# A 17-tap convolution by 48-point transforms of 32-node blocks, in batches of 16 graphs, in a two-layer graph network

## The chip, the cores and the metric

The kernel runs on one core of a Trainium2 chip, in one launch, all in f32. The time is that of the launch on the device in microseconds (us); the median of several runs is compared. PE is TensorE (matmuls), DVE is VectorE, ACT is ScalarE, POOL is GpSimd, and SP is the engine whose queue issues nearly all DMAs here.

## The reference

There are 64 graphs of 256 nodes with 256 features. Layer 0, with batch norms folded to a scale and a shift per channel:

```python
xc = transpose(x)                                   # channels x nodes
h = relu(bn1(conv1d(xc, conv1_w, taps=1)))
h = bn2(conv1d(h, conv2_w, taps=17, pad=8))         # along the nodes
x_conv = transpose(relu(h + xc))
s = x @ w_se.T + b_se                               # 3 numbers a node
A = exp(-(|s_n|^2 + |s_m|^2 - 2 s_n.s_m)) * adj
x_nmp = A @ relu(x @ w_msg.T + b_msg)
x_in = concat(x_conv, x_nmp)                        # 512 features
r, z, n = GRU gates of (x_in @ w_ih.T, x @ w_hh.T)  # sigmoid, sigmoid, tanh
x = layernorm(x + (1 - z) * n + z * x)
```

Layer 1 is `h = layernorm(x)`, `x + relu((adj @ h) @ W_rel + h @ W_root + b)`, and a last layernorm.

## The kernel before

**Pairs.** Graphs are worked on two at a time, 32 pairs. `pair(p)` loads the transposed x of both graphs (xT, line 1055) and the adjacency (adjm, 1058), makes messages (ps_msg, 1073) and distances (ps_dist, 1107), takes the exponential, multiplies it by the mask on VectorE (1114), and makes the neighbour sum nmp (1121). The conv result xc gets x added on VectorE (1127) and its relu on ScalarE (1128). Lines 1139 to 1142 form sums and differences of quarters of xT, nmp and xc on VectorE: the gate products (1155, by far the most of PE's work) are 2 x 2 block products done with 7 instead of 8 multiplications, except in the three pairs of `PLAIN`. Then follow the gates (1222 to 1231), transposes back (ps_wT, 1252), the norm's few small GpSimd operations (1265 to 1274), the projection (ps_hy, 1285), the aggregate (ps_agg, 1299) and the last norm (1310 to 1329). In the pairs of the last batch (`late`) the norms' sums come from VectorE's `bn_stats`; in others, from ScalarE with an accumulated output.

**The convolution** is done in batches of `BG` = 8 graphs. `conv1(b)` transposes x, stores it for later (xt), multiplies by conv1's matrix (828) and applies batch norm and relu (832). For batches after the first, the result goes to DRAM (hd) and comes back as XF (842). Each graph is cut into blocks of M = 16 nodes, and for each the T = 32 points of a cyclic transform over the block and its neighbouring nodes are taken: `fold` (767) makes the sums U and the differences V of halves, `split` (589 to 608) turns V and U down to points, each a pair re, im of [128 channels x 256] per channel half. At each of 15 complex points the conv is a product of 256 x 256 matrices, by three real products (lines 703 and 720 to 722): with the sum of re and im, with re, with im. Two real points need one each. That makes `NM` = 3 x 15 + 2 = 47 matrices. `merge` (619 to 643) and the last steps (878 to 886) go back up; ACT applies the second batch norm and writes the result to XC in SBUF (892).

The 47 matrices come from the 17 taps once, in `filters()`: a GpSimd copy lays 7 output channels together (ws, 538), PE turns them (544), multiplies by a constant matrix of cosines and sines (561, `NM * OB` = 329 columns), and ACT copies the result to W2 in SBUF (564). `store_w2` writes them to DRAM (w2m). Batch 0 multiplies straight from W2; later batches load three matrices a time (768 KB, line 696) into one of two places in `cs`.

**Order.** The program is first recorded as operations, each with a key (a wished time): `FIRST_GATES + p * PERIOD` for the gates of pair p, and a span of time over which the conv of the next batch is spread. `scheduled` plays a list schedule with estimated durations, giving each engine the ready operation with the lowest key, and the engines' queues are written in the order that comes out. It counts a DMA as 1.6 us plus its bytes by 205 KB/us, one after another. On the chip each engine runs its queue strictly in that order, SP too. PSUM has 8 banks, of which conv products may hold 3.

Of the kernel before, what the change touches and what calls it, by code (L numbers as in the profile page):

```python
# [18 lines left out]
P = 128  # L19
# [11 lines left out]
M, T = 16, 32  # L31
BG = 8
# [12 lines left out]
V0, U, S, S2, SLOTS = 0, 16, 32, 40, 48  # L45
HP_LEN = M * C * BG * (M + 1)

LEAVES = [(V0 + k, V0 + 8 + k, a) for k, a in enumerate(leaf_angles(PI / 2, 8))]
LEAVES += [(U + 8 + k, U + 12 + k, a) for k, a in enumerate(leaf_angles(PI / 2, 4))]
LEAVES += [(U + 4 + k, U + 6 + k, a) for k, a in enumerate(leaf_angles(PI / 2, 2))]  # L50
LEAVES += [(U + 2, U + 3, PI / 2)]
NM = 3 * len(LEAVES) + 2
SR, LR = 32, 100
OB = 7
HQ = 2 * M * C * (M + 1)
XC_SLOTS = BG + 2
FIRST_GATES, PERIOD, GATE_TIME = 143.0, 60.5, 18.0
AHEAD_FROM, AHEAD_TO, W_DEEP = -20.0, 10.0, 2
CONV1_FROM, CONV1_TO, CONV_FROM, CONV_OUT, CONV_TO = -10.0, 120.0, -6.0, -70.0, -30.0
PAIR_LEAD, FILTER_LEAD, LOAD_AHEAD = 20.0, 15.0, 12.0  # L60
# [3 lines left out]
def tap_matrix():  # L64

    k = np.arange(TAPS)
    cols = []
    for _, _, a in LEAVES:
        c, d = np.cos(k * a) / (T / 2), -np.sin(k * a) / (T / 2)
        cols += [c, d - c, c + d]  # L70
    cols += [np.ones(TAPS) / T, (-1.0) ** k / T]
    return np.stack(cols, 1).astype(np.float32)
# [177 lines left out]
DRAM_UNIT = P * D  # L250


def dram_cells(ap):

    name = ap.tensor.name
    if not name.startswith(("w2m", "xt", "hd")):
        return []
    dims = list(ap.ap)
    top = ap.offset + sum(s * (n - 1) for s, n in dims)
    return [(name, u) for u in range(ap.offset // DRAM_UNIT, top // DRAM_UNIT + 1)]  # L260

# [45 lines left out]
def scheduled(ops):  # L307
# [38 lines left out]
    while todo:  # L346
# [34 lines left out]
        if op.moved:  # L381
            dma = max(dma, now + 1.6) + op.moved / 205e3
# [23 lines left out]
def gnn_two_layers(  # L406
# [51 lines left out]
    cs = sb("cs", [P, W_DEEP * 3 * C * D])  # L458
    xn_ahead = sb("xn", [P, HQ])
    xn_ahead.base.fine = 0  # L460
    xTc_ahead = sb("xTc", [P, C, 2 * N])
# [5 lines left out]
    XF = sb("XF", [P, S * D + HP_LEN])  # L467
    XF.base.fine = S * D
    X = XF[:, :SLOTS * D].rearrange("p (s e) -> p s e", e=D)
    HP = XF[:, S * D:].rearrange("p (q j c g k) -> p q j c g k", q=BG // 2, j=M, c=C, g=2)  # L470
    w2m = tc.dram_tile([NM, C, P, D], F32, name="w2m")
    h_dram = tc.dram_tile([B // 2, 5, P, D], F32, name="hd")
    xt_dram = tc.dram_tile([B // 2, P, C, 2 * N], F32, name="xt")
    W2 = sb("w2all", [P, C, NM, D], "first")
# [31 lines left out]
    def store_w2(c):  # L506
        for f in range(0, NM, 8):
            g = min(f + 8, NM)
            SP.dma_start(out=w2m[f:g, c].rearrange("f p o -> p f o"), in_=W2[:, c, f:g, :])

    def filters():
        pieces, groups = [], []
        for c in range(C):
            for o0, o1 in ((0, 12 * OB), (12 * OB, 24 * OB), (24 * OB, D)):
                starts = [min(o, D - OB) for o in range(o0, o1, OB)]
                for a in range(0, len(starts), 4):
                    groups.append((len(pieces), starts[a:a + 4]))
                pieces.append((c, o0, o1))
        WT, TT = {}, {}
        WS, AHEAD = {}, 4  # L520
        wts = ring("wt", [P, TAPS, D - 24 * OB], 2, "filters")
        wss = ring("ws", [P, 4, TAPS, OB], AHEAD, "filters")
        tTs = ring("tT", [TAPS * OB, 4, P], 2, "filters")
# [29 lines left out]
        for i, (piece, starts) in enumerate(groups):  # L553
# [3 lines left out]
            if i + 1 < len(groups):  # L557
                TT[i + 1] = turned(i + 1)
            for a, o in enumerate(starts):
# [4 lines left out]
                A.copy(W2[:, c, :, o + skip:o + OB], pv[:, :, skip:])  # L564
# [47 lines left out]
    def merge(re, im, size, phi, scales, tmp, joint):  # L612
# [10 lines left out]
        else:  # L623
            joint = joint and h == 2
            for v in (slice(0, 2),) if joint else (0, 1):
                for j in range(2):
                    rho = scales[1][j] / scales[0][j]
                    a2, b2 = a[:, v, j::2], b[:, v, j::2]
                    stt(tt[:, v, j::2], b2, -rho, a2)
                    yield cost(h if joint else h // 2)  # L630
                    stt(a2, b2, rho, a2)
                    yield cost(h if joint else h // 2)
# [21 lines left out]
    TREES = [(V0, V0 + 8, 8), (U + 8, U + 12, 4), (U + 4, U + 6, 2)]  # L654
# [34 lines left out]
    w2_at = cycle(range(W_DEEP))  # L689

    def load_w(b, first, n):
        if b == 0:
            return lambda m, c: W2[:, c, first + m, :]
        at = next(w2_at) * 3 * C * D
        t = cs[:, at:at + 3 * C * D].rearrange("p (m c o) -> p m c o", m=3, c=C)
        SP.dma_start(out=t[:, :n], in_=w2m[first:first + n].rearrange("f c p o -> p f c o"))
        return lambda m, c: t[:, m, c, :]

    def product(ps, slot, w, m, first=True):
        with prog.group():  # L700
            for o in range(C):
                for c in range(C):
                    PE.matmul(ps[:, o * P:(o + 1) * P], w(m, c)[:, o * P:(o + 1) * P], X[:, slot, c * P:(c + 1) * P],  # L703
                              start=first and o == 0 and c == 0, stop=(c == C - 1), skip_group_check=True)

    def products(b, first, sums):
# [4 lines left out]
        for k in range(2):  # L711
            w = load_w(b, 3 * (first + k), 3)
            at = slice(k * D, (k + 1) * D)
            product(p1[:, at], sums + k, w, 0)
            product(p2[:, at], re + k, w, 1)
            product(p3[:, at], im + k, w, 2)

        def take():
            k1 = sl(sums, 2).rearrange("p s e -> p (s e)")
# [5 lines left out]
    def products_added(first, sums):  # L725
        p1, p3 = (bank(f"ps_k{i}", "conv") for i in (1, 3))
        re, im, _ = LEAVES[first]
        w = [load_w(0, 3 * (first + k), 3) for k in range(2)]
        at = [slice(k * D, (k + 1) * D) for k in range(2)]
        k1 = sl(sums, 2).rearrange("p s e -> p (s e)")  # L730
        for k in range(2):
            product(p1[:, at[k]], sums + k, w[k], 0, k == 0)
# [715 lines left out]
```

## Time and profile before

| what | us |
|---|---|
| median of 3 runs (2084.39 to 2088.04) | 2087.75 |
| the profiled execution's own time | 2085.32 |
| its span in the trace | 2083.5 |
| first gate matmuls (ps_g) in a run of their own | 151.4 |
| last DVE step of the first batch's conv (line 886) begins | 143.1 |
| conv products: records from `cs`, from W2 | 2632, 376 |
| SP waiting at line 1055 (load of xT) for DVE line 1229 | 220.5 |

The profile is one execution. Its page has the engines' busy shares, the span in 40 slices, the chain of work that ended last, groups of instructions by line and operation, and DMA issues. Further views are the timeline of an engine, the waits, and a table of busy time by stretches. An f32 matmul stands in the trace as two records.

### The profile page before, as it was taken

How to read it: one execution, taken by the hardware profiler on the slowest of the kernel's cores; microseconds unless marked ns; L12 is line 12 of the kernel's file. 1: busy time of each engine (PE TensorE's matmuls, PEld its weight loads, DVE VectorE, ACT ScalarE, POOL GpSimd, SP SyncE). 2: the span in 40 equal slices, each digit the busy share in tenths (PEclk: the TensorE clock that was granted, in tenths of full speed). 3: DMA queues.
4: the chain of work that ended last, by engine and by line, in shares of the span. 5: the costliest groups of instructions: out<-in, count | busy, mean ns of one | idle time of the engine just before them, and what ended most of it. 6: DMA issues, size and time to landing. Idle time of an engine off the chain costs nothing.

```text
span 2083.5 us, 28847 instructions
## 1 busy us (share of the span) xinstructions
PE 2048.0 (98%) x10492; PEld 1664.2 (80%) x10492; DVE 1685.8 (81%) x3028; ACT 1018.1 (49%) x2216; POOL 317.2 (15%) x555
## 2 busy tenths in 40 slices
PE   9989999999999999999999999999999999999996
PEld 6868779778887788878888788877888779887775
DVE  7983898899868998789868998689887899875644
ACT  7443433754447544564436544464445544365432
POOL 4100210122111201111101121112011220011101
PEclk9989999999999999999999999999999999999999
DMA  7734363334423244224433245232442225211100
GB/s 211 262 98 144 124 208 112 118 102 141 161 81 120 92 160 141 94 92 141 165 107 113 72 139 170 96 112 91 159 138 83 76 74 161 75 50 53 41 21 31
DMA packets 208201, 241.19 MB, mean 116 GB/s; under 512 B 23749, under 2 KB 192700, under 8 KB 208060
## 3 DMA queue, kind: packets, MB, share of 16 engines
q1 hardware_dynamic: 207518, 238.92, 35.6%
q8 instruction: 83, 1.36, 0.3%
q14 instruction: 58, 0.48, 0.1%
q10 hardware_dynamic: 542, 0.43, 0.1%
HBM read 177.85 MB, written 61.47 MB: 115 GB/s over the span
## 4 chain that ended last, share of the span: by engine, by line
PE 94%; DVE 4%; issue 1%; ACT 0%; POOL 0%; ACTq 0%; POOLq 0%; DVEq 0%
PE ps_a L1155 21%; PE ps_k L703 16%; PE ps_d L1155 11%; PE ps_hy L1285 11%; PE ps_msg L1073 5%; PE ps_agg L1299 5%; PE ps_c L828 5%; PE ps_b L1155 5%; PE ps_g L1155 5%; PE ps_nmp L1121 4%; PE ps_w L561 2%; PE ps_wT L1252 1%; PE ps_xTc L807 1%; PE ps_dist L1107 1%; DVE RG L1230 1%
## 5 line engine op out<-in xcount | busy, mean ns | idle before, releaser
L703 PEld LDWEIGHTS ps_k<-XF,cs 128*128 128x128 f32 x2632 | 313.2, 192 | 13.0 <-issue 6.6
L703 PE MATMUL ps_k<-XF,cs 128*128 128x128 f32 x2632 | 315.4, 275 | 0.0
L1285 PE MATMUL ps_hy<-wrr,wT 128*128 128x512 f32 x512 | 226.8, 595 | 0.0
L1285 PEld LDWEIGHTS ps_hy<-wrr,wT 128*128 128x128 f32 x512 | 96.6, 191 | 107.0 <-issue 102.1
L1169 ACT ACTIVATE RG<-ps_a,bhh 128x512 f32<-128x512 f32 x116 | 79.5, 686 | 191.0 <-PE ps_a L1155 129.4
L1155 PE MATMUL ps_a<-tx,WB 128*128 128x256 f32 x522 | 156.7, 382 | 0.0
L1167 ACT COPY ZN<-ps_a 128x512 f32<-128x512 f32 x116 | 67.6, 583 | 156.5 <-PE ps_a L1155 156.2
L1287 DVE SCALAR_TENSOR_TENSOR HY<-ps_hy,q,hrow 128x512 f32<-128x512 f32 x128 | 95.8, 749 | 55.8 <-PE ps_hy L1285 41.1
L675 DVE TENSOR_TENSOR XF<-XF 128x512 f32<-128x512 f32 (+3 forms) x128 | 126.4, 1010 | 5.3 <-ACT XF L756 3.0
L1073 PE MATMUL ps_msg<-wms,xT 128*128 128x260 f32 x512 | 124.7, 384 | 0.0
L1299 PE MATMUL ps_agg<-HY,adja 128*128 128x256 f32 x512 | 119.1, 380 | 4.0 <-issue 3.5
L1121 PE MATMUL ps_nmp<-AT,msg 128*128 128x256 f32 x512 | 118.8, 380 | 3.0 <-DVE AT L1114 3.0
L1299 PEld LDWEIGHTS ps_agg<-HY,adja 128*128 128x128 f32 x512 | 96.3, 190 | 31.3 <-issue 16.1
L1073 PEld LDWEIGHTS ps_msg<-wms,xT 128*128 128x128 f32 x512 | 95.3, 190 | 19.1 <-issue 5.8
L1121 PEld LDWEIGHTS ps_nmp<-AT,msg 128*128 128x128 f32 x512 | 95.4, 190 | 18.8 <-DVE AT L1114 4.2
L828 PE MATMUL ps_c<-xTc,w 128*128 128x512 f32 x232 | 107.7, 594 | 0.5 <-ACT xTc L808 0.5
L1155 PEld LDWEIGHTS ps_a<-tx,WB 128*128 128x128 f32 x522 | 95.1, 191 | 14.0 <-issue 1.5
L1155 PE MATMUL ps_a<-tc,WB 128*128 128x256 f32 x348 | 103.8, 380 | 0.0
L1155 PE MATMUL ps_a<-xc,WB 128*128 128x256 f32 x348 | 103.6, 379 | 0.0
L1155 PE MATMUL ps_a<-tn,WB 128*128 128x256 f32 x348 | 103.5, 379 | 0.0
L1155 PE MATMUL ps_a<-nmp,WB 128*128 128x256 f32 x348 | 103.5, 379 | 0.0
L1265 POOL TENSOR_SCALAR total<-total 128x4 f32<-128x4 f32 x28 | 15.5, 552 | 544.9 <-ACT x L1261 544.9
(213 smaller groups left out, 4642.7 us busy)
## 6 DMA issues: line engine op xcount, KB each, us to landing
cs<-w2m SPq DMA_DIRECT2D x105, 768.0 KB, 4.8
adjm<-in_adjT_dram SPq DMA_DIRECT2D x64, 256.0 KB, 2.8
xT<-xt SPq DMA_DIRECT2D x32, 512.0 KB, 3.7
adja<-in_adjT_dram SPq DMA_DIRECT2D x64, 256.0 KB, 2.7
out_dram<-HY SPq DMA_DIRECT2D x64, 256.0 KB, 2.1
hd<-xn SPq DMA_DIRECT2D x28, 544.0 KB, 3.2
XF<-hd SPq DMA_DIRECT2D x28, 544.0 KB, 4.0
xt<-xTc SPq DMA_DIRECT2D x29, 512.0 KB, 4.0
```

Source lines behind the costliest of these rows:

```text
L561: PE.matmul(ps[:, :NM * OB], TT[i][:, a, :], taps, start=True, stop=True)
L675: (V.tensor_add if add else V.tensor_sub)(sl(o, n), sl(a, n), sl(b, n))
L703: PE.matmul(ps[:, o * P:(o + 1) * P], w(m, c)[:, o * P:(o + 1) * P], X[:, slot, c * P:(c + 1) * P], start=first and o == 0 and c == 0, sto ...
L828: PE.matmul(ps, w1[:, c, o * P:(o + 1) * P], xTc[:, c, :], start=(c == 0), stop=(c == C - 1), hold=[h[:, :, o]])
L1073: PE.matmul(ps[:, :D + 4], xT[:, c, g, m * P:(m + 1) * P], wms[:, c, :], start=(c == 0), stop=(c == C - 1 and not idle), hold=[msg[:, g, m]])
L1121: PE.matmul(ps[:, d * N:(d + 1) * N], msg[:, g, m, d * P:(d + 1) * P], AT[:, g, m, :], start=(m == 0), stop=(m == C - 1), hold=[nmp[:, :, g]])
L1155: PE.matmul(ps[:, h * N:(h + 1) * N], block[:, s, gate, :], right[s][at], start=start and h == 0 and j == 0, stop=j == len(sources) - 1, s ...
L1167: A.copy(o, ps)
L1169: A.activation(o, ps, AF.Identity, bias=bhh[:, 2, f:f + 1])
L1285: PE.matmul(ps, wT[:, 2 * f + g, m * P:(m + 1) * P], wrr[:, f, :], start=(f == 0), stop=(f == C - 1), hold=[HY[:, g, m]], need=[q[:, 1, j: ...
L1287: stt(HY[:, g, m, :], ps, q[:, 1, j:j + 1], hrow)
L1299: PE.matmul(ps[:, n_ * D:(n_ + 1) * D], adja[:, g, m, n_ * P:(n_ + 1) * P], HY[:, g, m, :D], start=(m == 0), stop=(m == C - 1))
```

## The change

- Blocks of M = 32 nodes, T = 48 points, batches of 16 graphs: 4 batches for 8. With blocks of 32 and 16 nodes of neighbours, V has a tree of 16 complex points, U one of 7 complex and 2 real points. NM = 3 x 23 + 2 = 71. The transform's width stays 128 columns per channel half (16 graphs x 8 blocks for 8 x 16). `late` now covers 8 pairs, and conv runs beside the first 24 pairs.
- `fold` has 4 small operations and two more per graph pair for the middle nodes. HP, the place of the conv1 results, holds 3 graph pairs in turn instead of all.
- The last 26 matrices do not fit in W2 in SBUF. `filters` copies them to a small tile `wu` and stores them to DRAM; batch 0 loads them from there. Weights are now loaded one matrix (256 KB) at a time into three places in `cs`.
- `conv1` works on one graph at a time for batches after the first.
- The conv results go to DRAM (xc_dram), save for the first pair of each batch and pair 1, which go straight to XC; each pair loads its own 60 us ahead.
- x has three buffers, xTs, in place of two. Mask product, xc + xT and the differences of xT run on GpSimd.
- Constants of the order: FIRST_GATES 143 to 222, PERIOD 60.5 to 57.5, DMA rate 205 to 240 KB/us, and others.

```diff
-M, T = 16, 32
-BG = 8
+M, T = 32, 48
+TG = N // M
+BG = 16
...
-FIRST_GATES, PERIOD, GATE_TIME = 143.0, 60.5, 18.0
-AHEAD_FROM, AHEAD_TO, W_DEEP = -20.0, 10.0, 2
-CONV1_FROM, CONV1_TO, CONV_FROM, CONV_OUT, CONV_TO = -10.0, 120.0, -6.0, -70.0, -30.0
+HQ, HP_DEEP = 16 * C * (TG + 2) + HM, 3
+FILTERS_FROM, FILTERS_TO = 30.0, 110.0
+FIRST_GATES, PERIOD, GATE_TIME = 222.0, 57.5, 18.0
+AHEAD_FROM, AHEAD_TO, W_DEEP = -79.0, -5.0, 3
+CONV1_FROM, CONV1_TO, CONV_FROM, CONV_OUT, CONV_TO = -10.0, 230.0, -6.0, -59.0, -20.0
+STORES, WB_AT = (82.0, 115.0), 7.0
...
-            dma = max(dma, now + 1.6) + op.moved / 205e3
+            dma = max(dma, now + 1.6) + op.moved / 240e3
...
-    cs = sb("cs", [P, W_DEEP * 3 * C * D])
+    xos = ring("xo", [P, 2, N], 2)
+    cs = sb("cs", [P, W_DEEP * C * D])
...
-                A.copy(W2[:, c, :, o + skip:o + OB], pv[:, :, skip:])
+                A.copy(W2[:, c, :, o + skip:o + OB], pv[:, :NV, skip:])
+                A.copy(wu[:, :, o + skip - o0:o + OB - o0], pv[:, NV:, skip:])
+            if i + 1 == len(groups) or groups[i + 1][0] != piece:
+                SP.dma_start(out=w2m[NV:, c, :, o0:o1].rearrange("f p o -> p f o"), in_=wu[:, :, :o1 - o0])
...
-    def load_w(b, first, n):
-        if b == 0:
-            return lambda m, c: W2[:, c, first + m, :]
-        at = next(w2_at) * 3 * C * D
-        t = cs[:, at:at + 3 * C * D].rearrange("p (m c o) -> p m c o", m=3, c=C)
-        SP.dma_start(out=t[:, :n], in_=w2m[first:first + n].rearrange("f c p o -> p f c o"))
-        return lambda m, c: t[:, m, c, :]
+    def load_w(b, f):
+        if b == 0 and f < NV:
+            return W2[:, :, f, :]
+        t = next(leaves_w[b > 0])
+        SP.dma_start(out=t, in_=w2m[f].rearrange("c p o -> p c o"))
+        return t
...
+        for w, r in ((0, 8), (1, 0)):
+            hv = ends(h)[:, :, w].rearrange("p g j c k -> p (j c) g k")
             for first, op in ((V0 + r, ALU.subtract), (U + r, ALU.add)):
+                V.tensor_tensor(into(first, 8).rearrange("p s (g t) -> p s g t", t=TG), hv[:, :, :, 1 - w:TG + 1 - w],
+                                hv[:, :, :, 2 - w:TG + 2 - w], op)
+        for g in range(2):
+            at = slice(g * TG, (g + 1) * TG)
+            stt(into(V0 + 16, 16)[:, :, at], middle(h)[:, g].rearrange("p j c t -> p (j c) t"), 2.0,
+                into(U, 16)[:, :, at], op1=ALU.subtract)
...
+                kept = XC[p % 2][:, o] if at_once(p) else next(xos)
+                A.activation(kept.rearrange("p g (t j) -> p j (g t)", j=M),
+                             X[:, V0:V0 + M, o * P + 2 * q * TG:o * P + 2 * (q + 1) * TG], AF.Identity,
+                             bias=bn_shift[1][:, o:o + 1], scale=bn_scale[1][:, o:o + 1])
+                if not at_once(p):
+                    SP.dma_start(out=xc_dram[p, o], in_=kept.rearrange("p g n -> p (g n)"))
...
-    xTs = [sb(f"xT{i}", [P, C, 2, N], "ahead") for i in range(2)]
+    xTs = [sb(f"xT{i}", [P, C, 2, N], "ahead") for i in range(3)]
+    spare = xTs[2].rearrange("p c g n -> p (c g n)")
+    leaves_w += [cycle(matrices(cs) + matrices(spare)), cycle(matrices(cs))]
...
-            V.tensor_mul(AT[:, g], AT[:, g], adjm[:, g])
+            G.tensor_mul(AT[:, g], AT[:, g], adjm[:, g])
...
+        if not at_once(p):
+            prog.at(due - 60)
+            SP.dma_start(out=xc.rearrange("p c g n -> p c (g n)"), in_=xc_dram[p].rearrange("c p e -> p c e"))
-        V.tensor_add(xc, xc, xT)
+        G.tensor_add(xc, xc, xT)
...
+            E = G if v is xT else V
-            V.tensor_sub(t1, b12, b11)
-            V.tensor_sub(t2, b22, t1)
-            V.tensor_sub(t4, b21, t2)
-            V.tensor_sub(t3, b22, b12)
+            E.tensor_sub(t1, b12, b11)
+            E.tensor_sub(t2, b22, t1)
+            E.tensor_sub(t4, b21, t2)
+            E.tensor_sub(t3, b22, b12)
```

## The prediction

> **What bounds the kernel now.** I read the engines' shares first, then the slices, the chain that ended last, and the longest groups of that chain.
>
> ```profile
> PE 2048.0 (98%) x10492; PEld 1664.2 (80%) x10492; DVE 1685.8 (81%) x3028; ACT 1018.1 (49%) x2216; POOL 317.2 (15%) x555
> PEclk9989999999999999999999999999999999999999
> PE 94%; DVE 4%; issue 1%; ACT 0%; POOL 0%; ACTq 0%; POOLq 0%; DVEq 0%
> L703 PE MATMUL ps_k<-XF,cs 128*128 128x128 f32 x2632 | 315.4, 275 | 0.0
> ```
>
> TensorE is busy in 98% of the span, makes up 94% of the chain, and runs at full clock but for one slice near the start. Busy alone does not prove a full engine, since a matmul's recorded 0.28 to 0.6 us overlaps its neighbours. So I take the time from the start of one matmul to the start of the next (the timeline of PE):
>
> ```profile
> 506.10 2.84 PE L703 MATMUL ps_k<-XF,cs 128*128 128x128 f32 x24
> 508.78 1.88 PE L828 MATMUL ps_c<-xTc,w 128*128 128x512 f32 x4
> 510.50 1.05 PE L703 MATMUL ps_k<-XF,cs 128*128 128x128 f32 x8
> 511.39 0.38 PE L1098 MATMUL ps_sT<-ident,sts 128*100 128x128 f32 x2
> 61.88 2.38 PE L561 MATMUL ps_w<-taps,tT 119*128 119x329 f32 x8
> 64.10 0.60 PE L544 MATMUL ps_tT<-ident,ws 128*119 128x128 f32 x4
> ```
>
> A 128-column matmul holds PE for (508.78-506.10)/24 = 0.112 us, a 512-column one for 1.72/4 = 0.43, a 329-column one for 2.22/8 = 0.277: 0.83 ns a column and 3 to 5 ns over. A 256-column one takes 0.216 in the same view. Adding such slots over the whole timeline fills about 2030 of 2083.5 us; of the rest some 21 us lie in the first 160 us and 11 in the last 43. In between PE has hardly a gap. **So a matmul taken out is time taken out, unless a new wait fills the hole.** The table by stretches says the same, and how near the others are (columns: stretch, its length, then PE, PEld, DVE, ACT, POOL busy, clock, DMA share, GB/s):
>
> ```profile
> 0.00:140.00 140.00, 136.32 (x770) 105.73 (x770) 114.70 (x170) 77.43 (x168) 34.54 (x54) 1.00 0.67 201
> 140.00:160.00 20.00, 14.71 (x47) 9.46 (x48) 15.78 (x24) 11.47 (x18) 0.31 (x2) 0.66 0.22 79
> 723.00:1703.00 980.00, 974.25 (x5066) 800.68 (x5066) 841.82 (x1521) 489.22 (x1083) 150.22 (x256) 1.00 0.36 117
> 1860.00:2040.00 180.00, 177.96 (x791) 142.54 (x790) 103.33 (x213) 78.62 (x153) 20.55 (x51) 1.00 0.14 43
> ```
>
> The third row holds 16 pairs (pair 8's first ps_hy matmul starts at 723.8, pair 24's at 1702.9): 61.2 us of PE a pair and 52.6 of DVE (86%).
>
> **The matmuls, term by term.** A batch of the conv multiplies one matrix per transform point product: 3 x 15 + 2 = 47 now, 3 x 23 + 2 = 71 after. Each is 4 matmuls, recorded as two f32 passes: 8 records of 128 columns. Now: 8 batches x 47 x 8 = 3008 (2632 from cs and 376 from w2all). After: 4 x 71 x 8 = 2272. 736 x 0.1117 = **-82.2 us**.
> Filters: the same 148 matmuls at L561, with NM x OB = 497 columns for 329. 168 x 0.833 ns = 0.14 us each: **+20.7 us**, all in the startup.
> conv1 for batches 1 to 3 goes graph by graph: 48 x 8 records of 256 columns at 0.216 = 82.9 us for 24 x 8 at 0.43 = 82.6: +0.4. Transposes, gates and the rest of a pair are as before.
> PE sum: -82.2 + 20.7 + 0.4 = **-61 us**. By stage: 10.5 us of the 61.2 a pair are products and 4.3 conv1, so 46.4 are the pair. After, 568 x 0.1117 / 8 = 7.9 a pair are products: 58.7 us in the first 16 pairs, 54.3 in the next 8 (no conv1), 46.4 in the last 8 (no conv; before, only the last 4).
>
> **What may take it back: startup.** Twice the graphs are transformed before the first gates. Count DVE in slots of 256 elements per partition. Now: fold 32, split of V 72, sums 8, split of U 67, reads of PSUM 16, merges 102, last steps 46 = 343. After: 48 + 192 + 16 + 67 + 24 + 222 + 62 = 631. Now it took about 115 us of DVE (114.70 to time 140, with the last steps ending at 143.7), 0.335 us a slot; so 211 after. DVE begins at 14, and idled 15; conv1 of 8 graph pairs feeds it one pair per 4.4 us of PE against 2.1 of folding, so some 9 more idle: 14 + 211 + 24 = 249, and 7 to the first gates as now (143.7 to 151): near 256 for 151. PE has, before that, filters 69.8, conv1 of two batches 69, products 63.4, preparation of pairs 0 and 1 at 12.4 each, and warm-up and row sums of 9: 236 us. So about 20 us of PE idle, with some lower clock behind it, for 21 now. ACT, with a second copy per filter group (w2all at 0.459 us per 329 elements becomes 315 + 182, 0.755 for 74 blocks = 56; tT copies 12; conv1 28), has 96 us against PE's 104 there (now 58 against 66): close, but covered. I take **+8 us**; ends -10 (gap closed) and +35 (conv1 of batch 1 misses its place, 34.6 us of PE).
>
> **GpSimd beside DVE.** Seven operations a pair (mask 2 x 512 elements, xc+xT 1024, differences of x 4 x 256) leave DVE, 4.3 us by its rows. The trace has no large two-input operation on GpSimd. What it has is its copy in the startup, and what DVE did meanwhile:
>
> ```profile
> 47.73 0.68 DVE L606 SCALAR_TENSOR_TENSOR XF<-XF 128x512 f32<-128x512 f32 x1
> 47.92 3.02 POOL L538 COPY ws<-wt 128x476 f32<-128x476 f32 x3 [2.07 <-PE ps_tT L544]
> 48.44 0.99 DVE L608 SCALAR_TENSOR_TENSOR XF<-XF 128x512 f32<-128x512 f32 x1
> 49.36 1.10 DVE L606 SCALAR_TENSOR_TENSOR XF<-XF 128x512 f32<-128x512 f32 x1
> 50.49 0.99 DVE L608 SCALAR_TENSOR_TENSOR XF<-XF 128x512 f32<-128x512 f32 x1
> 51.41 0.68 DVE L606 SCALAR_TENSOR_TENSOR XF<-XF 128x512 f32<-128x512 f32 x1
> ```
>
> The DVE operation of 0.68 us takes 0.99 to 1.10 beside three copies of 1.0 us; start to start the four stand 0.71, 0.92, 1.13 and 0.92 apart, for 0.60 alone: 1.28 us lost in 3.02. So what moves to GpSimd is not free for DVE. At the copy's 2.1 ns an element the 3072 elements are 6.5 us of GpSimd a pair; with two inputs, at most twice, 13. DVE loses about 0.4 us per us of it in the fence: 2.6, at worst all 13. Conv itself on DVE: 980 us in its rows / 32 = 30.6 a pair now; after, 653 slots x 0.267 + 333 operations x 0.147 = 223 per 16 graphs, 27.9 a pair. DVE a pair: 52.6 - 2.7 - 4.3 + 2.6 = 48 of 58.7 and of 54.3 us; at the worst 58.6, over in the middle stage by 4.3 x 8 = 34. On GpSimd the new operations stand ahead of the small ones of the norm (L1265 to L1322), a few us before x1 and the output; PE has other pairs' matmuls there. I take **+3**, ends 0 and +35.
> [...]
>
> **Weights.** Now cs holds two groups of 3 matrices, after three single ones (and W2 lacks 26 of 71, which batch 0 reads back).
>
> ```profile
> cs<-w2m SPq DMA_DIRECT2D x105, 768.0 KB, 4.8
> adja<-in_adjT_dram SPq DMA_DIRECT2D x64, 256.0 KB, 2.7
> ```
>
> A 256 KB load lands 2.7 us after issue, and is issued when the product three places earlier has ended. Two products between are 1.8 us. So three products on end stall PE by about 1 us, unless over 1 us of other matmuls lies among them. The scheduler counts 2.7 us for such a load and places products when it expects them, but SP also blocks in order: behind a weight load that waits stand xT, adjm, xc. I take **+8**, ends 0 and 71 x 1 = +71 over three batches. The third x buffer takes SP's wait for L1229 (220 us in the waits of SP) off the queue; PE never waited for it, so 0. The conv results through DRAM: 57 stores of 256 KB and 28 loads of 512 KB, 30 MB on a queue at 36%: hidden, 60 us ahead of use; 0.
>
> **Last stage.** 8 pairs, not 4, run with no conv to fill gaps, with statistics on DVE. The fourth stretch row shows some 2 us not busy in 180 us. **+5**, ends 0 and +15.
>
> **Sum.** -61 + 8 + 3 + 8 + 5 = -37. Against the profiled execution's own 2085.32 us: 2048; the median of the runs is 2.4 above it, so 2050.7, say **2050**. Faster by 38 us, 1.8%.
>
> **Rivals.** (1) *Nothing given back*: the -61 whole, 2026. For it: PE went without a gap through stages with DVE at 86%. Against: the startup count. Chance 0.17. (2) *Startup exposed*: PE idles for conv1's 35 us more as well as the small terms, and GpSimd's block costs part of its 35: 2066 to 2083, about 2075. For it: the 6.3 us idle at 137.8 and the 0.66 clock behind it, in the same place now. Against: PE has 236 us of work there. Chance 0.16. (3) *Slower*: products run on end and wait for their weights, nearly 1 us in three products over batches 1 to 3, 71 us, with the other terms (16) it is +26: 2114. For it: the chain now has ps_k in runs of 48, six products on end, again and again. Against: a product is needed only every 4 us of a stage. It decides from two thirds of the triples stalling. Chance 0.13. (4) *No change*: half of that, with the startup's loss, 0.04. The forecast, 2035 to 2066, has 0.50.
> Range: from 2024 (rival 1 less 2) to 2084 (rival 2 whole). It leaves out (3), most of (4) and a little below: under 0.2. About 0.2% (4 us) is what a measurement tells from no change: faster 0.50 + 0.17 + 0.16 = 0.83, same 0.04, slower 0.13.
>
> **What would show it.** Right: 2272 ps_k records at 0.112 slots, ps_w at 0.417; first gates near 250 with PE nearly full before; pairs 58 to 60 us apart, then 54 to 56, then 47 to 49; no PE wait for cs. Wrong: PE waits for DMA cs<-w2m; a PE gap of over 30 us before the gates; DVE at 95% in the third stage with PE waiting for XF, xc or AT.

## The result, and the profile after

The changed kernel takes 2177.0 us (median of 4 runs, 2176.5 to 2179.0) against 2087.7 before: ratio 1.0433, 95% interval 1.0415 to 1.0451. It is slower by 89 us; the forecast was 38 us faster. The profiled execution took 2176.5 us with a span of 2174.6.

The same views as before, now of the kernel after: engines, clock, shares of the chain, and the group of products.

```profile
PE 2037.6 (94%) x9948; PEld 1638.3 (75%) x9948; DVE 1611.8 (74%) x2689; ACT 1012.5 (47%) x2240; POOL 554.9 (26%) x713
...
PEclk9889879999999999999999999999999999999998
...
PE 62%; DVE 24%; DMA 5%; ACT 3%; issue 3%; SPq 2%; POOL 2%; ACTq 0%; DVEq 0%; POOLq 0%
...
L729 PE MATMUL ps_k<-XF,cs 128*128 128x128 f32 x1800 | 223.4, 276 | 3.2 <-DVE XF L698 1.6
```

TensorE has less work (9948 matmul records for 10492) and is no longer the whole chain: 62% for 94%. VectorE makes up 24% for 4, DMA 5% for nothing. The granted clock (PEclk) dips in the startup's slices, in the sixth to 0.7. PE's timeline in the filters:

```profile
64.96 0.49 PE L559 MATMUL ps_tT<-ident,ws 128*119 128x128 f32 x3
70.07 4.25 PE L579 MATMUL ps_w<-taps,tT 119*128 119x497 f32 x6 [4.62 <-ACT tT L561]
74.16 0.49 PE L559 MATMUL ps_tT<-ident,ws 128*119 128x128 f32 x3
74.49 2.67 PE L579 MATMUL ps_w<-taps,tT 119*128 119x497 f32 x6
76.99 0.49 PE L559 MATMUL ps_tT<-ident,ws 128*119 128x128 f32 x3
```

Undisturbed, six filter matmuls take 2.50 us from start to the next group's start (74.49 to 76.99): 0.417 a piece, as forecast. The group at 70.07 waited 4.6 us first, and its six took 4.09 to the next start; from 69.7 to 73.1 us the granted clock was 0.50 (the eighth number below):

```profile
69.70:73.10 3.40, 3.03 (x4) 1.51 (x5) 3.37 (x3) 2.79 (x9) 0.00 (x0) 0.50 1.35 61
```

Now the stretches (length; PE, PEld, DVE, ACT, POOL busy with counts; clock, DMA share, GB/s): two of the startup, the tail of it before the first gates, and the three stages of 8 pairs with conv but their ends.

```profile
60.00:160.00 100.00, 72.51 (x227) 38.67 (x225) 59.12 (x67) 41.91 (x134) 15.57 (x16) 0.83 1.24 123
160.00:260.00 100.00, 91.00 (x656) 82.98 (x654) 84.20 (x130) 33.87 (x78) 11.34 (x11) 0.95 0.77 240
260.00:307.00 47.00, 32.66 (x89) 19.75 (x88) 39.84 (x54) 16.41 (x40) 10.66 (x9) 0.63 0.63 197
307.00:827.00 520.00, 504.59 (x2563) 421.09 (x2562) 396.38 (x669) 271.59 (x589) 125.07 (x155) 0.99 0.41 131
827.00:1287.00 460.00, 440.76 (x2276) 366.33 (x2276) 372.57 (x603) 219.09 (x517) 133.23 (x156) 1.00 0.38 118
1287.00:1747.00 460.00, 435.66 (x2178) 358.99 (x2177) 392.40 (x648) 206.03 (x464) 131.35 (x158) 0.98 0.32 96
```

In the first row the DMA engines' busy share reads 1.24 and they move only 123 GB/s; in the second, with a share of 0.77, 240. The three stages have PE idle for 15 to 25 us each; before's two stages from 723 to 1703 us had under 6 together.

To put sizes on this I count PE in slots, as the prediction did (0.83 ns a column and 3 to 5 ns per matmul), and call the rest idle. The columns are bounded by the first ps_hy matmul of pairs 0, 8, 16 and 24. "Length" is per pair of a stage. Slots and idle time add up to 6 to 9 us more than each span, about alike for all, because some matmuls start a little sooner than a slot behind the last. A row is of the one profiled execution; that of e3_both was the fastest of its ten, 6 us below its median.

| kernel | slots, us | idle: startup | stage 1 | stage 2 | stage 3 | stage 4 | length of stages 1, 2, 3 |
|---|---|---|---|---|---|---|---|
| before | 2023 | 22 | 9 | 6 | 14 | 18 | 63.6, 61.2, 61.2 |
| after | 1963 | 93 | 31 | 37 | 37 | 21 | 62.5, 61.7, 57.7 |
| e1_all_on_dve | 1963 | 94 | 14 | 23 | 32 | 16 | 60.9, 59.5, 57.4 |
| e2_wide_rows | 1963 | 41 | 29 | 37 | 37 | 21 | 62.3, 61.8, 57.7 |
| e3_both | 1963 | 45 | 15 | 16 | 34 | 16 | 60.7, 58.4, 57.6 |
| v1_wide_dve | 1963 | 44 | 18 | 17 | 35 | 17 | 61.3, 58.2, 57.8 |
| v1_less_dve | 1963 | 46 | 19 | 10 | 24 | 17 | 61.2, 59.2, 55.3 |

So the matmuls lost 60.6 us of slots, the forecast's -61. PE's idle time grew by some 152 us, of which 72 lie in the startup, 22, 31 and 23 in the three stages with conv and 3 in the last. Net: +91, the difference of the two spans.

### The profile page after: what moved, and what is told of

Same layout as the page of the kernel before. It is cut to its first block, busy times and chain, and to the rows that moved or that the text cites. A ratio compares the mean times of both kernels' runs of the same rounds, so it can differ in the third digit from the quotient of the medians.

```text
span 2174.6 us, 28409 instructions
## 1 busy us (share of the span) xinstructions
PE 2037.6 (94%) x9948; PEld 1638.3 (75%) x9948; DVE 1611.8 (74%) x2689; ACT 1012.5 (47%) x2240; POOL 554.9 (26%) x713
## 4 chain that ended last, share of the span: by engine, by line
PE 62%; DVE 24%; DMA 5%; ACT 3%; issue 3%; SPq 2%; POOL 2%; ACTq 0%; DVEq 0%; POOLq 0%
PE ps_a L1218 15%; PE ps_hy L1348 10%; PE ps_k L729 8%; PE ps_d L1218 6%; PE ps_agg L1362 4%; PE ps_g L1218 4%; PE ps_b L1218 4%; PE ps_c L868 3%; DMA w2m<-wu 3%; PE ps_msg L1132 2%; DVE RG L1293 2%; DVE RG L1292 2%; DVE XF L627 2%; PE ps_nmp L1180 2%; DVE wT L1294 2%
## 5 line engine op out<-in xcount | busy, mean ns | idle before, releaser
L729 PEld LDWEIGHTS ps_k<-XF,cs 128*128 128x128 f32 x1800 | 220.4, 192 | 12.2 <-DMA cs<-w2m 2.4
L729 PE MATMUL ps_k<-XF,cs 128*128 128x128 f32 x1800 | 223.4, 276 | 3.2 <-DVE XF L698 1.6
L1189 POOL TENSOR_TENSOR xc<-xc,xT 128x1024 f32<-128x1024 f32 x32 | 83.0, 2595 | 248.9 <-DMA xc<-xq 65.5
L1132 PE MATMUL ps_msg<-wms,xT 128*128 128x260 f32 x512 | 133.3, 396 | 6.8 <-DMA xT<-xt 3.5
L1173 POOL TENSOR_TENSOR AT<-AT,adjm 128x512 f32<-128x512 f32 x64 | 95.6, 1511 | 149.1 <-ACT AT L1170 149.0
L1180 PE MATMUL ps_nmp<-AT,msg 128*128 128x256 f32 x512 | 123.3, 385 | 4.9 <-POOL AT L1173 4.9
L874 ACT ACTIVATE xn<-ps_c,bnsh,bnsc 128x128 f32<-128x128 f32 x192 | 76.5, 463 | 59.4 <-PE ps_c L868 35.6
```

What stands on the lines that cost most here:

```text
L729: PE.matmul(ps[:, o * P:(o + 1) * P], w[:, c, o * P:(o + 1) * P], v[:, c * P:(c + 1) * P], start=first and o == 0 and c == 0, stop=(c == C ...
L874: A.activation(to, v, AF.Relu, bias=bn_shift[0][:, o:o + 1], scale=bn_scale[0][:, o:o + 1])
L1132: PE.matmul(ps[:, :D + 4], xT[:, c, g, m * P:(m + 1) * P], wms[:, c, :], start=(c == 0), stop=(c == C - 1 and not idle), hold=[msg[:, g, m]])
L1173: G.tensor_mul(AT[:, g], AT[:, g], adjm[:, g])
L1180: PE.matmul(ps[:, d * N:(d + 1) * N], msg[:, g, m, d * P:(d + 1) * P], AT[:, g, m, :], start=(m == 0), stop=(m == C - 1), hold=[nmp[:, :, g]])
L1189: G.tensor_add(xc, xc, xT)
```

## Experiments

Ratios are against the kernel before in the same runs (2084.7 to 2085.5 us).

### What holds up the startup, and what the stages

**Theory 1:** the operations moved to GpSimd hold VectorE up, and delay those who wait for either. **Rival 2:** it is the conv's own merges on VectorE, which come in bunches. For the startup: **A**, the stores of the last 26 matrices in rows of 168 bytes (42 columns of f32) clog the DMA engines; **B**, VectorE sets the first gates.

**e1_all_on_dve.** After, with the seven operations of a pair back on VectorE.

```diff
-            G.tensor_mul(AT[:, g], AT[:, g], adjm[:, g])
+            V.tensor_mul(AT[:, g], AT[:, g], adjm[:, g])
...
-        G.tensor_add(xc, xc, xT)
+        V.tensor_add(xc, xc, xT)
...
-            E = G if v is xT else V
+            E = V
```

> The changed kernel with the mask, xc + xT and the differences of xT back on VectorE; all else as changed. Theory 1 (GpSimd's two-input operations hold up VectorE, and PE then waits for the gates' elementwise chain): the stretched VectorE operations (105 us of extra duration between 320 and 1830 us) go, the waits of PE for wT and ZN shrink from 50 us to under 20, pairs stand 59 to 60 us apart in the first two stages for 62 now, and the time is near 2105 us (2085 to 2125). Theory 2 (the larger transform tree bunches its merges on VectorE, whoever does the mask): VectorE has 4 us more a pair, PE waits as much or more, 2165 to 2200 us.

Measured: 2141.7, ratio 1.0285 (1.026 to 1.0309), 35 us below after: Theory 1's direction, but about half of the gain that it expected (2085 to 2125). In the timeline of after, GpSimd and VectorE stand beside each other like this (GpSimd first):

```profile
899.52 2.25 POOL L1173 TENSOR_TENSOR AT<-AT,adjm 128x512 f32<-128x512 f32 x1
901.74 1.70 POOL L1202 TENSOR_TENSOR tx<-xT 128x256 f32<-128x256 f32 x1
903.52 1.58 POOL L1203 TENSOR_TENSOR tx<-xT,tx 128x256 f32<-128x256 f32 x1
905.06 0.90 POOL L1205 TENSOR_TENSOR tx<-xT 128x256 f32<-128x256 f32 x1
...
912.95 3.19 POOL L1189 TENSOR_TENSOR xc<-xc,xT 128x1024 f32<-128x1024 f32 x1 [1.66 <-DMA xc<-xq]
```

```profile
898.35 2.29 DVE L627 SCALAR_TENSOR_TENSOR XF<-XF 128x1024 f32<-128x1024 f32 x1
900.68 2.17 DVE L629 SCALAR_TENSOR_TENSOR XF<-XF 128x1024 f32<-128x1024 f32 x1
...
904.44 0.94 DVE L1202 TENSOR_TENSOR tc<-xc 128x256 f32<-128x256 f32 x1
905.41 0.83 DVE L1203 TENSOR_TENSOR tc<-xc,tc 128x256 f32<-128x256 f32 x1
...
911.22 1.22 DVE L629 SCALAR_TENSOR_TENSOR XF<-XF 128x1024 f32<-128x1024 f32 x1
...
913.83 2.59 DVE L614 SCALAR_TENSOR_TENSOR XF<-XF 128x256 f32<-128x256 f32 x1
916.34 0.41 DVE L616 SCALAR_TENSOR_TENSOR XF<-XF 128x256 f32<-128x256 f32 x1
```

The 1024-element step that takes 1.22 us alone takes 2.29 and 2.17; the 256-element one takes 0.94, and 2.59 beside the 3.19 us addition, for 0.41. The long ones end about one operation behind the end of the GpSimd operation beside them (901.77 + 1.1, and 916.14 + 0.3; the first, too, ends 1.1 behind 899.5, where the next GpSimd operation starts): it looks as if the two take turns. GpSimd is slowed too: its 256-element difference takes 1.70 and 1.58 where others of the same form take 0.90. Taking each VectorE operation against the usual time of its form, between 320 and 1800 us VectorE loses 101 us in after, 6 in before, 4.6 in e1: about 4.2 us a pair, nearly all that it was relieved of (4.3). Its busy time over the whole run says the same, 1611.8 us in after and 1607.5 in e1. The move took nothing off VectorE and added a delay on both. Where that reaches PE is in its waits from 320 to 1800 us, of after and then of e1 (columns: total, times, longest):

```profile
PE ps_wT L1315 <- DVE wT L1294: 30.8, 22, 3.7
PE ps_d L1218 <- DVE ZN L1236: 13.8, 8, 3.0
...
PE ps_nmp L1180 <- POOL AT L1173: 4.9, 1, 4.9
...
PE ps_k L729 <- DMA cs<-w2m: 1.6, 3, 0.8
```

```profile
PE ps_a L1218 <- ACT RG L1232: 17.6, 7, 5.1
...
PE ps_wT L1315 <- DVE wT L1294: 3.1, 1, 3.1
```

PE waited 31 us for the gates' last step on VectorE (wT), 22 times, and now 3. Theory 1 holds in the stages: e1 takes 17, 14 and 4 us of idle time out of them, and 5 out of the last. In return e1 has a wait for ScalarE (RG, 17.6 us) that is not among those of after. That this is delay and not VectorE's amount of work is seen in its share over the first two stages: 769 of 980 us in after, 788 of 970 in e1, more and yet faster. The startup is as it was (the first gates at 308.1 for 306.7).

**e2_wide_rows.** After, with the same bytes of the last 26 matrices stored in rows of 1 KB in place of 168 bytes; the numbers of these matrices stand in other places by it.

```diff
...
-                SP.dma_start(out=w2m[NV:, c, :, o0:o1].rearrange("f p o -> p f o"), in_=wu[:, :, :o1 - o0])
+                k4 = NV + o0 // (6 * OB) * 4
+                SP.dma_start(out=w2m[k4:k4 + 4, c].rearrange("f p o -> p f o"), in_=flat_wu[:, :4 * D].rearrange("p (f o) -> p f o", o=D))
...
```

> The changed kernel, but the last 26 matrices are stored to DRAM in whole rows of 1 KB instead of rows of 42 floats (168 bytes): as many bytes at the same places in the order, but the numbers in them are then in the wrong place, so the conv of the late points is not the reference's. Theory A (the small rows clog the DMA queue, filters wait for their taps and for wu): filters end near 120 us for 153, first gates near 275 for 307, time near 2147 us (2135 to 2160). Theory B (twice the startup work on VectorE sets it): filters may end sooner but the first gates move by less than 8 us, 2168 to 2180 us.

Measured: 2122.8, ratio 1.0177 (1.0162 to 1.0192), 54 us below after. The DMA issues of after and of e2 (times, KB each, median us from issue to landing):

```profile
w2m<-w2all SPq DMA_DIRECT2D x10, 1024.0 KB, 12.6
w2m<-wu SPq DMA_DIRECT2D x10, 546.0 KB, 13.9
...
wt<-in_w2T_dram SPq DMA_DIRECT2D x10, 357.0 KB, 8.2
```

```profile
w2m<-w2all SPq DMA_DIRECT2D x10, 1024.0 KB, 8.1
w2m<-wu SPq DMA_DIRECT2D x12, 512.0 KB, 3.5
...
wt<-in_w2T_dram SPq DMA_DIRECT2D x10, 357.0 KB, 5.7
```

Nearly the same bytes a store land in 3.5 us instead of 13.9, and the other stores and the loads of the taps, queued with them, are quicker too. In the first 260 us e2's rows are (60 to 160, the stretch shown above for after):

```profile
60.00:160.00 100.00, 100.00 (x546) 71.19 (x545) 98.35 (x128) 56.05 (x162) 22.83 (x21) 1.00 0.77 236
```

PE is full and at full clock, where it was busy 72.5 us at 0.83. The last filter matmul starts at 112.2 (after: 152.2), the first gates come at 249.2 (after: 306.7); both, and the time, are better than what was expected of Theory A. In after, PE's waits from 40 to 310 us had this at the top, ScalarE's over the whole run have the next line, and VectorE's from 60 to 170 only the last:

```profile
PE ps_w L579 <- ACT tT L561: 27.5, 6, 6.5
PE ps_hrow L1085 <- DMA wrr<-in_wroot_dram: 11.5, 1, 11.5
```

```profile
ACT wu L583 <- DMA w2m<-wu: 45.8, 9, 9.6
```

```profile
DVE nmp L897 <- DMA w2m<-w2all: 45.9, 1, 45.9
```

PE waits for ScalarE, but ScalarE waits for a free wu tile, and the chain through this stretch alternates between these stores and SP. A name in PE's wait is the last link only. VectorE stood 46 us still: its sums go to nmp and xT, places that open only when the filters' tiles are all stored. Theory A, then, and not B: 53 of the startup's 72 us.

Rows of 168 bytes took 4 times as long as rows of 1 KB (13.9 us for 546 KB, 3.5 for 512), and rows of 512 bytes (v1_wide_dve, below) were not slow: 1664 KB in 8.0 us. How the narrow ones are slow, no run here shows.

**e3_both.** Both edits.

> Both edits at once (all on VectorE, whole rows; the late points' matrices hold wrong numbers). Theories 1 and A: the gains add, near 2073 us (2055 to 2095), so below the kernel before. Theories 2 and B: 2160 to 2195 us. Theory 1 with B: near 2100; theory 2 with A: near 2145.

Measured: 2089.8, ratio 1.0016 (1.0004 to 1.0029), 87 us below after: the two add up (35 + 54). The expectation was near 2073 (2055 to 2095). This is before's time, with 61 us less matmul work. So some 57 us of idle time are still there: 23 in the startup, 6, 10 and 20 in the stages.

**e4_before_gpsimd.** The kernel before with the seven operations on GpSimd, e1's edit the other way round.

> The kernel before, with the mask, xc + xT and the differences of xT moved to GpSimd, and nothing else changed. Theory 1: VectorE operations are stretched by some 4 us a pair, PE waits for the gates' elementwise chain, 2120 to 2180 us. Theory 2: VectorE is relieved by 4 us a pair, PE stays full, 2075 to 2095 us.

Measured: 2112.4, ratio 1.0131 (1.0116 to 1.0146): +27 us on a kernel with no other change. Its groups on GpSimd:

```profile
L1114 POOL TENSOR_TENSOR AT<-AT,adjm 128x512 f32<-128x512 f32 x64 | 88.1, 1397 | 266.8 <-ACT AT L1111 264.3 <-DMA out_dram<-HY 2.4
L1127 POOL TENSOR_TENSOR xc<-xc,xT 128x1024 f32<-128x1024 f32 x32 | 85.9, 2685 | 189.2 <-DMA xT<-xt 170.2 <-DMA xn<-in_x_dram 12.4 <-ACT xc L892 6.6
```

2.6 to 2.7 ns an element, 8.5 us a pair with the differences (the prediction had 6.5 to 13). The time lies between the ranges of the two theories (2075 to 2095, and from 2120). But VectorE's operations lose 101 us between 320 and 1800 us here too, for 6 in before, and PE's waits for wT, ZN and AT there add up to 23 us for 6. So Theory 1 stands without any of the conv's change, at a smaller price than expected.

**e5_gpsimd_cost.** After, with the scheduler's estimate of a GpSimd operation raised to what was measured. **1a:** the order was laid out with too short times; **1b:** the turn-taking itself costs.

```diff
-                dur = 1.5 if ALU.pow in args else 0.45 + 1.5e-3 * n
+                dur = 1.9 if ALU.pow in args else 0.35 + 2.5e-3 * n
```

> The changed kernel, but the scheduler counts a GpSimd operation at 0.35 us + 2.5 ns an element (1.9 us for the power) for 0.45 + 1.5: what the trace shows. Theory 1a (PE loses because results from GpSimd come later than the order was laid out for): the loss by GpSimd, 35 us, shrinks to under 15, 2150 to 2162 us. Theory 1b (VectorE is blocked while GpSimd reads, which the estimate does not hold): within 10 us of the changed kernel, 2167 to 2187.

Measured: 2181.8, ratio 1.0464 (1.0448 to 1.0479). No gain, as 1b expected; 1a falls.

### Where the other 57 us are

**v1_wide_dve** undoes both with the conv's numbers as they should be: all on VectorE; wu holds 128 columns (rows of 512 bytes, four stores of 1664 KB that land in 8.0 us); tiles not used in the filters' time move to the pool "ahead" to make room, and the loads of wrr and hrow, which PE had waited for, go before those of the gate weights. **C:** what is left is VectorE near its limit, in the third stage above all. **D:** it is ScalarE, whose writes of conv results come in a bunch and wait for their stores.

```diff
-STORES, WB_AT = (82.0, 115.0), 7.0
+STORES, WB_AT = (82.0, 115.0), -25.0
...
-DRAM_UNIT, W_PIECE = P * D, 6 * OB
+DRAM_UNIT, W_PIECE = P * D, D // 2
...
-        rest = ring("wu", [P, NM - NV, D - 30 * OB], 2, "filters")
+        rest = ring("wu", [P, NM - NV, D // 2], 2, "filters")
...
```

> The changed kernel with three edits: all elementwise work back on VectorE; the last 26 matrices stored in rows of 128 columns (512 bytes), the numbers all in their places (tiles that are idle in the filters' time move to make room); and the loads of wrr and hrow ahead of those of WB, all some 30 us earlier in the order. If the rows' width and GpSimd are the two large causes, as the runs with both undone say (2090 us), and the 9.4 us that PE waited for wrr there are the next one, this is near 2080 us (2068 to 2092). If 512-byte rows are still narrow, filters end later and it stays near 2105.

Measured: 2088.0, ratio 1.0015 (1.0006 to 1.0025), where 2080 was expected (2068 to 2092). Below, this version is called v1.

**v1_less_dve** leaves out the mask product and xc + xT, but in the three plain pairs.

> As the kernel with the three edits, but the mask product and xc + xT are left out of all but the three plain pairs: A is not masked and the conv lacks its residual. VectorE has 2.6 us a pair less. Theory C (what remains of the loss is VectorE, near its limit when a batch's folds and splits are done with the pairs, most in the third stage): the pairs of the third stage stand 55 to 56 us apart for 57.6, the holes of PE at the stage boundaries shrink, 20 to 40 us faster than with them. Theory D (it is ScalarE's bunched writes of the conv results, or the loads): less than 8 us faster.

Measured: 2071.7, ratio 0.9936 (0.9921 to 0.995): -16 us for 2.6 us a pair taken off VectorE, between what Theory C (20 to 40) and Theory D (under 8) expected. Of the idle time 7 us went from the second stage and 11 from the third, none from the others. The stretches about the third stage of v1_wide_dve, and then the middle one of this:

```profile
1240.00:1320.00 80.00, 76.80 (x334) 60.51 (x333) 71.56 (x111) 39.32 (x87) 14.62 (x18) 1.00 0.27 87
1320.00:1420.00 100.00, 86.19 (x416) 68.10 (x415) 89.00 (x154) 37.82 (x90) 15.51 (x24) 0.95 0.25 74
1420.00:1720.00 300.00, 294.88 (x1540) 246.30 (x1539) 234.35 (x446) 147.03 (x327) 42.97 (x74) 0.99 0.33 102
```

```profile
1320.00:1420.00 100.00, 92.12 (x476) 75.06 (x476) 94.11 (x172) 42.02 (x103) 17.11 (x28) 0.97 0.33 98
```

VectorE is the busier engine in both, and with a little work less PE gets 60 matmuls more done beside it. This speaks for C in about half of the third stage's loss (its pairs are 55.3 us apart, 55 to 56 expected). It does not part VectorE's amount of work from the shorter way to the gates that leaving the two steps out also makes.

**v1_two_x_four_xo** tests D: two x buffers, and four places for the conv results on their way to DRAM in place of two. Its partner is **v1_two_x**, with two x buffers alone, which prices the third.

> As the kernel with the three edits, but with two x buffers as before (and so three places for batch 0's weights, not five). The prediction put the third buffer at 0: within 6 us. If the load of x, behind the wait of SP for the last use of its buffer, also held up the weights behind it: 10 to 30 us slower.

> As v1_two_x (2106: two x buffers), with four places in place of two for the conv results on their way to DRAM. Theory D (ScalarE's bunched writes of the conv results wait for their stores and hold ScalarE and then TensorE up at the end of every batch): 8 to 15 us below v1_two_x, 2092 to 2098. Theory C (VectorE, not these writes): within 4 us of 2106.

Measured: v1_two_x 2106.1, ratio 1.0093 (1.0074 to 1.0111); v1_two_x_four_xo 2111.2, ratio 1.0117 (1.0102 to 1.0133). Four places gain nothing, 5 us more where D expected 8 to 15 less, and ScalarE's waits for these stores add up to only 7.0 us in v1_two_x: D falls. And the third x buffer is worth 18 us to v1, where the prediction had 0. 20 us more of idle time stand in the startup: first gates at 274 for 261. The third buffer also gives batch 0 two of its five places for the matrices read back from DRAM (10 of the 26 loads go there), and pair 2 its x; which of the two makes the 18 us was not tried.

**v1_no_split** leaves the split of V out of batch 0, an estimated 62 us of VectorE's work (59 less up to the first gates in the trace); the results of batch 0 are others by it. **B':** with the rows wide, VectorE's amount of work sets the first gates. **A':** the filters and their stores still do.

> As v1_wide_dve, but batch 0 leaves out the split of V (192 slots of 256 elements of VectorE's 631 in the startup, some 62 us; the results of batch 0 are others by it). Theory B' (in v1 VectorE's chain of transforms alone sets the first gates, 262 us): the first ps_hy comes 40 to 62 us earlier than v1's 326 as far as TensorE's own 236 us of work there allow, so about 240 for the gates, and the time falls by the 20 to 25 us that TensorE idled there more than before: about 2066. Theory A' (filters and their stores set it even with the wide rows): first gates within 8 us of v1's and the time within 6 of 2088.

Measured: 2089.9, ratio 1.0024 (1.0015 to 1.0033); first gates 260.1 for 260.9. Nothing moved, so B' falls. The rows of v1_no_split show why (before the filters' end at 111, and from there to the last product of batch 0):

```profile
60.00:111.00 51.00, 51.00 (x160) 26.08 (x160) 11.89 (x19) 41.99 (x130) 8.69 (x16) 1.00 0.83 224
111.00:214.00 103.00, 93.89 (x693) 84.83 (x692) 70.76 (x112) 30.89 (x69) 3.21 (x6) 0.98 0.83 259
```

VectorE is idle for 39 of the 51 us ahead of the filters' end: whatever it saves there, PE is full with the filters, and a product needs them all. Up to there VectorE's work is hidden. In the second row it has 21 us less to do than in v1 (70.76 for 91.78, below), and that moved nothing either.

**v1_less_merge** leaves out the last two operations of every merge of batch 0 instead, an estimated 26 us behind the filters' end. **S:** filters and VectorE's merges stand in series. **P:** PE's own work and its order set the gates.

> As v1_wide_dve, but batch 0 leaves out the last two operations of every merge, some 26 us of VectorE's work behind the filters' end at 111 us (the results of batch 0 are others by it). Theory S (in series: the filters have to end before the first product, and VectorE's merges follow; work ahead of the filters' end is hidden, as v1_no_split showed, work behind it is not): first gates 15 to 26 us earlier than v1's 261, and 12 to 20 us off the time: 2068 to 2076. Theory P (TensorE's own 113 us of work behind the filters, and its order, set the gates): gates within 6 us of 261, time 2084 to 2092.

Measured: 2083.6, ratio 0.9993 (0.9983 to 1.0002); first gates 253.2, 8 us earlier for 24 us less on VectorE (the rows below). Between the two, nearer to P. The stretches from the filters' end to the last product, and from there to the gates: before, v1_wide_dve, v1_less_merge.

```profile
72.00:127.00 55.00, 55.00 (x430) 50.31 (x429) 47.42 (x74) 15.11 (x35) 2.55 (x5) 1.00 0.49 161
127.00:149.00 22.00, 15.46 (x56) 7.63 (x54) 17.76 (x30) 14.02 (x24) 2.77 (x7) 0.85 0.65 206
```

```profile
111.00:215.00 104.00, 94.79 (x706) 85.42 (x705) 91.78 (x143) 32.87 (x74) 2.24 (x6) 1.00 0.82 257
215.00:261.00 46.00, 32.26 (x128) 23.27 (x127) 43.51 (x63) 24.28 (x55) 2.80 (x5) 0.84 0.65 216
```

```profile
111.00:213.00 102.00, 93.60 (x697) 84.02 (x696) 76.68 (x113) 32.58 (x73) 2.54 (x6) 1.00 0.82 258
213.00:253.00 40.00, 29.93 (x104) 19.91 (x103) 34.95 (x55) 17.11 (x41) 2.58 (x5) 0.75 0.61 200
```

The startup is three links in series. The filters end at 111. The last product of batch 0 comes at 214.8, 213.6 and 213.4 in the three versions of v1, whatever VectorE has to do: PE is over 90% busy there, with conv1 of batch 1 and the first pairs' preparation laid among the products. Then the merges and last steps behind the last product run on VectorE, 46 us (40 with less merging) where before took 22, while PE has little that is ready, and that at a clock of 0.84 (0.75 with less merging; before: 0.85). PE's idle time in the startup grew by 22 us from before to v1. Counted in slots, it is 23 us in this tail (before: 11) and 14 between the filters and the last product (before: 3), so about half of the growth is the longer tail. Less merging shortened the tail by 6 us, but left PE's idle time in it at 22.

**Four other orders** of v1: v1_gates_250 (first gates wished at 250, period 58.5), v1_gates_250_p57 (250, 57.5), v1_gates_262_p59 (262, 59), and v1_period_60 (222, 60). Only wished times differ; conv1 of batch 1 begins, and the gate weights are loaded, at the same wished times as in v1.

> As v1_wide_dve with the order laid out for first gates at 250 in place of 222 and a period of 58.5 in place of 57.5 (measured in v1: 262, and 61.3, 58.3 and 57.8 by stage); the work is the same. If part of the 62 us still lost comes from an order made for times the chip does not keep: 2070 to 2080. If it is VectorE's amount of work: 2084 to 2092, as 2088.

> As v1_wide_dve with a period of 60 in place of 57.5 in the order's wished times alone, so that conv work is spread a little later against the gates. Order at fault: 2072 to 2082, with the spacing of pairs in the third stage under 57. VectorE's amount of work: 2084 to 2092.

> As v1_gates_250 (2082.9) with the period of 57.5 back. If it was the later gates that gave v1_gates_250 its 5 us: 2080 to 2086. If it was the longer period: 2086 to 2092, as v1_wide_dve.

> As v1_wide_dve with the order laid out for the measured gates (262) and a period of 59. If matching the order to the chip's times gains: 2074 to 2082. If the third stage is bound by VectorE's amount of work whatever the order: 2082 to 2092.

| kernel | median, us | ratio, 95% interval |
|---|---|---|
| v1_gates_250 | 2082.9 | 0.9982 (0.997 to 0.9994) |
| v1_gates_250_p57 | 2096.3 | 1.0045 (1.003 to 1.006) |
| v1_gates_262_p59 | 2094.2 | 1.004 (1.0027 to 1.0054) |
| v1_period_60 | 2094.5 | 1.0036 (1.0024 to 1.0048) |

Neither the later gates nor the longer period gains by itself, and wishing for what was measured (262) doesn't either; these three are slower than either theory expected (at most 2092). None of the wished times tried wins the 57 us back. They move the time within 13 us with no direction. This is also a measure for the other versions of v1: each of their edits changes the order that the scheduler lays out as well, so that the differences of 2 to 5 us among them can't be told from a change of order, and 16 and 18 us are not far above it. v1_gates_250 is the one version with the whole computation that is below before, by 2 us, about what can be told from no change.

## Why the prediction was wrong

By its own steps:

- **Matmuls, -61: right.** 2272 ps_k records at 0.112 us from start to start, the filters at 0.417; slots 60.6 us less.
- **Startup, +8 (ends -10, +35): the step that failed most, at +72.** It counted PE, VectorE and ScalarE and never priced the startup's DMAs. The 26 matrices that don't fit got a term for their copies on ScalarE and a word in passing as batch 0's reads; the 12 stores that put them in DRAM had none, though the code gives their rows: 42 columns, 168 bytes (46 columns in two of them). They cost 53 us (e2).
- **The rest of that step.** VectorE's sum was right: 211 us forecast, and v1 has 215 to the time 255, about 10 of it the first pairs' work, and the first gates come at 249 to 261 where the stores are wide, 256 forecast. But the sum ran over the whole startup as if PE's 236 us of work could lie anywhere beside it. Work ahead of the filters' end hides under PE, work behind the last product doesn't: that tail grew from 22 to 46 us. With it, and with what it lost between the filters and the last product, PE lost 22 us in v1's startup, where the term was 8.
- **GpSimd, +3 (ends 0, +35): mis-sized, at +35** by e1, +27 by e4. The upper end was the right one. VectorE lost 4.2 us a pair where 2.6 was taken: GpSimd was at work for 8.9 us a pair where 6.5 was taken, and the loss was 0.47 us per us of it, near the fence's 0.4. The larger error is that the sum was made in busy time, 48 of 58.7, where the price is delay: the stretched steps are among those that the gates' last step, and PE behind it, wait for. In the stretch shown one waited for most of the other: a 0.41 us operation took 2.59 beside an addition of 3.19, and ended 0.3 us behind it. No run shows the worst case from which the upper end was made (rival 2's "GpSimd's block"), VectorE losing all of 13 us a pair: it lost 4.2 beside 8.9 of GpSimd.
- **Third stage, 54.3 us a pair forecast: 57.6 with both causes undone.** VectorE was counted at 48 us of it on average; in v1 it is at 89% around the stage's start (1240 to 1420 us), where PE idles for 17 us, and at 78% in the next 300. A mean over a stage hid that, as it did in the startup. The stage's extra idle time is some 20 us, of which v1_less_dve recovers 11; that VectorE causes the rest is not shown.
- **Weights, +8 (ends 0, +71): near 2.** PE waits for cs 1.6 us in three times from 320 to 1800 us. Rival 3 of the prediction (slower, 2114) had the sign by luck, with a mechanism that did not occur. Rival 2 of the prediction named both places that lost, the startup and GpSimd beside VectorE, but put no more than PE's 35 us of conv1 on the first. The count of the conv results' transfers was a little off (54 stores and 27 loads, for 57 and 28).
- **Third x buffer, 0: mis-sized**, worth 18 us in v1, with the reserve about orders made above. PE's waits of before could not show it; the change's own lines do (`spare` and `leaves_w`, which let batch 0 use the buffer for weights).
- **Last stage, +5: near at +3, by luck.** With the seven operations back on VectorE (e1, e3, v1) the stage idles for 16 or 17 us, less than before's 18. So the missing conv and the statistics, which the term was for, cost nothing to be seen, and the 3 us go with GpSimd.

Of the signs named as wrong, "a PE gap of over 30 us before the gates" came (in sum: PE idle 50 us from 60 to 307), PE's wait for cs did not, and VectorE was at 85% in the third stage, not 95.

So the steps that failed are the startup, whose stores had no price and whose work was summed as if it could lie anywhere, GpSimd's delay, and the mean over the third stage. What stays open: of the third stage's 20 us, 9 are in v1_less_dve still, and stages 1 and 2 keep 16 us more idle time than before in e3_both; no run took these apart. Why the turn-taking costs 35 us here and 27 in the kernel before was not tried either.

## What to carry over

Price every DMA that a change adds by the length of its rows as well as its bytes (here 13.9 us for 3.5, at 168 bytes a row for 1 KB), above all in a stage where PE can't do without it. An engine's busy sum over a stage says little: put the work in order (what must end before what) and look for the links that run alone. Moving elementwise work to GpSimd beside a busy VectorE took nothing off VectorE here: a pair, 4.3 us were moved and 4.2 lost.

## What the runs showed of the hardware

- Stores of SBUF to DRAM in rows of 168 bytes: 546 KB land in 13.9 us; in rows of 1 KB, 512 KB in 3.5; in rows of 512 bytes, 1664 KB in 8.0 (after, e2, v1; medians). The narrow ones slow what is queued beside them: 1 MB of wide rows 12.6 us for 8.1.
- An f32 operation with two inputs on GpSimd, beside a busy VectorE, took 2.5 to 3.0 ns an element (means of 512 and 1024 elements, after and e4), and a VectorE operation that began 0.9 us into one of 3.19 us ended 0.3 us behind it (2.59 us for 0.41; after).
- TensorE's granted clock was below full in the stretches of after's startup where it idled in part: 0.95 at 91% busy, 0.83 at 73%, 0.63 at 69%. It was 1.00 at 91% in v1's from 111 to 215 us, so the share alone does not set it. Behind a wait of 4.6 us, with a granted clock of 0.50 for most of their time, six filter matmuls took 4.09 us from start to start for 2.50. So PE at a lowered clock did less work than its busy time says: from 260 to 307 us of after, at 0.63, the matmuls fill 19 us of slots and are recorded as 32.7 us busy.
